# Layer 0 of a four-layer graph network: a fourth buffer for a tile's own rows, and the scatter of a tile's finished rows written inside the next tile's loop over runs

## The chip, the cores and the metric

The kernel runs on one core of a Trainium2 chip. The metric is the device time of one execution, in microseconds (us), given as the median of several executions. The engines are named as the profile names them: PE multiplies matrices, DVE works on vectors, ACT applies activations and copies, POOL issues the indexed transfers here, and SP issues the plain ones. Each engine takes its instructions in one fixed order that is settled when the program is built, and waits on semaphores for the others.

## The reference, cut to what matters

3125 nodes with rows of 128 numbers pass through four graph layers over the same 100000 edges; after each layer the result is added to its input and normalised. The layer that is touched here is the first, an attention layer with 8 heads:

```python
pre_edge = hP1[dst] + hP2[src] + zP3[edge_type]
logit_edge = _leaky(pre_edge) @ y_w
...
alpha = ex / denom[dst_a]
t_edge = hWh[src] + zWz[edge_type]
msg = (alpha[:, :, None] * t).reshape(-1, D)
agg = jax.ops.segment_sum(msg, dst_a, num_segments=n)
out = _leaky(agg + residual_weight * h)
x = _layernorm(x + out)
```

Each node also attends to itself; `denom` is the softmax's sum over a node's incoming edges and itself.

## The kernel before, in words

Nodes are sorted by their number of incoming edges and cut into 25 tiles of 128. A tile's edges fill `CAP[t]` slots for each node, from 57 in the first tile to 21 in the last, and the slots are worked in chunks of up to eight; consecutive chunks form a run.

Layer 0 loops over the tiles t:

1. `own(t + 1)` (L796) fetches the next tile's own rows: POOL clears a buffer `x` (L798) and issues an indexed gather into it (L799, recorded under the helper's line L102). Rows beyond the real nodes stay zero. There are three such buffers, so the memset of tile t + 3 needs the buffer of tile t back. The last to read `x` of tile t is the DVE instruction at L1024, which forms `y`.
2. For every chunk POOL issues up to eight gathers of neighbours' rows, `hs`, one for each slot (L102). Eight `hs` buffers are in use in turn. A chunk of the "gathered" kind also gathers rows of the relation table, `zs`, with two buffers; a chunk of the "multiplied" kind gets them from PE, by matmuls with one-hot matrices (L870, L879). PE adds the parts of the argument of the leaky function (L821, L883, L885), ACT applies it (L828), PE makes logits (L830).
3. After each run DVE does the softmax and the weighted sum (L904 to L914). This piece is given a high priority by `tc.high_priority(offset=AHEAD)`. Its last add, L914, gives the chunk's `hs` buffer back.
4. A tail finishes the tile: the node's attention to itself, `y` (L1024), the normalised rows `x1` (L757, in a helper; two `x1` buffers), and `put` (L105 in the helper `scatter`), an indexed scatter of the 128 rows into the table `x1_tab`, issued by POOL. Then `x1` is transposed and multiplied for layer 1.

Between the chunks the loop also hands out steps of another task, `counts`, which builds matrices of edge counts for layer 1 on DVE, ACT and PE.

The order of the instructions on each engine is not the order of the source. A scheduler goes through the source order with priorities, places an instruction when by its own reckoning its inputs and its buffer are free, and so lets POOL run ahead: it places the gathers of tile t + 2 before the scatter of tile t. What it placed is then fixed, and POOL waits in that order. All table writes of `put` are declared free of mutual order, since their nodes differ. Layer 1 and the later layers start when layer 0 has ended.

Of the kernel before, what the change touches and what calls it, by code (L numbers as in the profile page):

```python
# [8 lines left out]
F32 = mybir.dt.float32  # L9
# [9 lines left out]
P = 128  # L19
N = 3125  # L20
NT = 25
# [7 lines left out]
D = 128  # L29
# [58 lines left out]
def tile_gnn(ctx, tc, a, out):  # L88
# [12 lines left out]
    def gather(dst, table, idx, **kw):  # L101
        return G.indirect_dma_start(out=dst, out_offset=None, in_=table, in_offset=indirect(idx), **kw)  # L102

    def scatter(table, idx, src, **kw):
        return G.indirect_dma_start(out=table, out_offset=indirect(idx), in_=src, in_offset=None, **kw)  # L105

    def unordered(group, inst, reason):

        tc.declare_no_dep(inst.ins, group=group, reason=reason)
        tc.add_to_no_dep_group(group, inst.ins)  # L110
# [365 lines left out]
    od = Order("d", order_d)  # L476
# [287 lines left out]
    def put(table, o, t, rows):  # L764
        unordered(f"rows_{table.name}", scatter(table, o.ids(t), rows), "nodes differ")

    x1_tab = dram.tile([NP, D], F32, name="x1_tab")
# [8 lines left out]
    with tc.tile_pool(name="l0", bufs=2) as wp, tc.tile_pool(name="l0s", bufs=1) as sp, \  # L776
# [14 lines left out]
        def sums_of(t):  # L791
            az = wp.tile([P, D + R], F32, name="az")
            nc.sync.dma_start(az, sums_at[t])
            return az[:, :D], az[:, D:], az

        def own(t):  # L796
            x = wp.tile([P, D], F32, name="x", bufs=3)
            G.memset(x, 0.0)  # L798
            gather(x, a["x"], od.ids(t), bounds_check=N - 1, oob_is_err=False)  # L799
            return x  # L800

        def prologue(t, x):

            xT = transposed(wp, ps1, x, "xT", "misc")
            pw = ps1.tile([P, D + HC + H], F32, name="pw", tag="misc")
            T.matmul(pw, xT, w0, start=True, stop=True)
            hw = wp.tile([P, D + HC + H], F32, name="hw")
            A.activation(hw, pw, AF.Copy)
            hq = wp.tile([P, 3, D], BF16, name="hq")
            A.activation(hq[:, 0, :], pw[:, :D], AF.Copy)  # L810
            hrest = wp.tile([P, D], F32, name="hrest")
            V.tensor_sub(hrest, pw[:, :D], hq[:, 0, :])
            A.activation(hq[:, 1, :], hrest, AF.Copy)
            V.tensor_sub(hq[:, 2, :], hrest, hq[:, 1, :])
            return hw, hq
# [119 lines left out]
        steps = all_counts()  # L935
        n_steps = sum(4 + -(-CAP[t] // SG) + NCW for t in range(NT))
        done = 0.0
        x1st = own(0)
        ahead = x1st, prologue(0, x1st)
        for t in range(NT):  # L940
            n = CAP[t]
            x, (hw, hq) = ahead
            if t + 1 < NT:
                x_next = own(t + 1)
            ac, za, _ = sums_of(t)
            lg_ps = ps1.tile([P, max(CAP), H], F32, name="lg")
            zbT = wp.tile([P, P], F32, name="zbT")
            unset = True
            for run in runs(t):
                hss = []  # L950
                for s0, w, mult in run:
                    o = OFF[t] + s0
                    if s0 + w == n and t + 1 < NT:

                        ahead = x_next, prologue(t + 1, x_next)
                    if mult:
                        hs = multiplied(hq, o, w, zbT, unset, lg_ps[:, s0:s0 + w])
                        unset = False
                    else:
                        hs = gathered(hq, lambda s: srcx[:, o + s:o + s + 1], rel[:, o:o + w], w, za,  # L960
                                      lg_ps[:, s0:s0 + w])
                    hss.append((s0 - run[0][0], w, hs))

                    done += n_steps * w / NS
                    while done > 0:
                        next(steps, None)
                        done -= 1

                s0, s1 = run[0][0], sum(run[-1][:2])
                with tc.high_priority(offset=AHEAD):  # L970
                    lg = masked(lg_ps[:, s0:s1], hss, s1 - s0, mask[:, OFF[t] + s0:OFF[t] + s1])
                    corr, rest = weights(wp, lg[:, :s1 - s0], s1 - s0, H, m[:, t, :], l[:, t, :])
                    faded(ac, corr, H)
                    for q, w, hs in hss:
                        spread(ac, hs, lg[:, q:q + w], w)
                    rest()


            zaT_ps = ps1.tile([P, P], F32, name="tp", tag="misc")
            T.transpose(zaT_ps[:R], za, ident)  # L980
            zaT = wp.tile([R, P], F32, name="zaT")
            A.activation(zaT, zaT_ps[:R], AF.Copy)
            zb_ps = ps1.tile([P, 2 * D], F32, name="zb_ps", tag="misc")
            T.matmul(zb_ps, zbT, zw[:, :2 * D], start=True, stop=False)
            T.matmul(zb_ps, zaT, zw[:R, :2 * D], start=False, stop=True)
            zb = wp.tile([P, 2 * D], F32, name="zb")
            V.tensor_scalar(zb, zb_ps, od.rdeg[:, t:t + 1], None, op0=OP.mult)
            self_ = wp.tile([P, 2 * D], F32, name="self")
            V.tensor_add(self_, hw[:, D:3 * D], zb)
            V.tensor_add(self_[:, :D], self_[:, :D], hw[:, :D])  # L990
            V.scalar_tensor_tensor(self_[:, :D], self_[:, :D], 0.2, self_[:, :D], op0=OP.mult, op1=OP.max)
            sT = transposed(wp, ps1, self_[:, :D], "xT", "misc")
            sl_ps = ps1.tile([P, H], F32, name="sl_ps", tag="misc")
            T.matmul(sl_ps, sT, yw, start=True, stop=True)

            sl = wp.tile([P, H], F32, name="sl")
            V.tensor_sub(sl, sl_ps, hw[:, D + HC:])
            mf = wp.tile([P, 3, H], F32, name="mf")
            V.tensor_max(mf[:, 0, :], sl, m[:, t, :])
            V.tensor_sub(mf[:, 1, :], sl, mf[:, 0, :])  # L1000
            V.tensor_sub(mf[:, 2, :], m[:, t, :], mf[:, 0, :])
            A.activation(mf[:, 1:, :], mf[:, 1:, :], AF.Exp)
            V.tensor_mul(l[:, t, :], l[:, t, :], mf[:, 2, :])
            V.tensor_add(l[:, t, :], l[:, t, :], mf[:, 1, :])
            rl = wp.tile([P, H], F32, name="rcl")
            V.reciprocal(rl, l[:, t, :])
            V.tensor_mul(mf[:, 1:, :], mf[:, 1:, :], rl.unsqueeze(1).to_broadcast([P, 2, H]))

            def heads(ap):
                return ap.rearrange("p (h d) -> p h d", h=H)  # L1010

            ts = self_[:, D:]
            V.tensor_mul(heads(ac), heads(ac), mf[:, 2, :].unsqueeze(2).to_broadcast([P, H, D // H]))
            V.tensor_mul(heads(ts), heads(ts), mf[:, 1, :].unsqueeze(2).to_broadcast([P, H, D // H]))
            V.tensor_add(ac, ac, ts)
            V.scalar_tensor_tensor(ac, x, rw, ac, op0=OP.mult, op1=OP.add)
            V.scalar_tensor_tensor(ac, ac, 0.2, ac, op0=OP.mult, op1=OP.max)
            has = wp.tile([P, 2], F32, name="has")
            V.tensor_scalar(has[:, 0:1], od.deg[:, t:t + 1], 0.0, None, op0=OP.is_gt)
            V.tensor_scalar(has[:, 1:2], od.deg[:, t:t + 1], 0.0, 1.0, op0=OP.is_le, op1=OP.add)  # L1020

            V.tensor_scalar(ac, ac, has[:, 0:1], None, op0=OP.mult)
            y = wp.tile([P, D], F32, name="y")
            V.scalar_tensor_tensor(y, x, has[:, 1:2], ac, op0=OP.mult, op1=OP.add)  # L1024
            x1 = wp.tile([P, D], F32, name="x1")
            layernorm(wp, x1, y, t)
            put(x1_tab, od, t, x1)

            x1T = transposed(wp, ps1, x1, "xT", "misc")
            u_ps = ps1.tile([P, D], F32, name="u_ps", tag="misc")  # L1030
            T.matmul(u_ps, x1T, w1T, start=True, stop=True)
            u3 = wp.tile([P, 3, D], BF16, name="u3")
            A.activation(u3[:, 0, :], u_ps, AF.Copy)
            rest = wp.tile([P, D], F32, name="rest")
            V.tensor_sub(rest, u_ps, u3[:, 0, :])
            V.tensor_copy(u3[:, 1, :], rest)
            V.tensor_sub(u3[:, 2, :], rest, u3[:, 1, :])
            nc.sync.dma_start(u_tab[:, t * 3 * D:(t + 1) * 3 * D], u3.rearrange("p k d -> p (k d)"))
# [361 lines left out]
```

## Time and profile before

| | us |
|---|---|
| median of 3 runs | 5517.07 (5515.46 to 5533.62) |
| profiled execution, its own time | 5534.14 |
| its span | 5532.3 |
| layer 0's loop over tiles, in the span | about 204 to 2760 |
| POOL busy in the span | 2781.5 |
| gathers of `hs`: 821, busy | 834.9 |
| gathers of own rows: 25, busy | 30.9 |
| memsets of `x`: 25, busy | 5.2 |
| scatters into `x1_tab`: 25, busy | 31.6 |

The profile is of one execution. For each group of instructions it gives the busy time and the idle time of the engine just before, with the instruction that ended the wait (the releaser). "Issue" stands for idle time in which no wait is seen to end. On POOL the busy time of a transfer is that of issuing it. In the profile's names digits are cut off, so `x1` stands as `x`, and `x1_tab` as `x_tab`; `x_tab<-x` is the scatter and `x<-in_x` the gather of own rows.

### The profile page before, as it was taken

To read this page: it belongs to the slowest core of one execution; us is meant where nothing else is said; L and a number is where in the kernel's file an instruction comes from. 1 tells how busy PE (TensorE), PEld (TensorE's weight loads), DVE (VectorE), ACT (ScalarE), POOL (GpSimd) and SP (SyncE) were. 2 spreads that over 40 slices of the span, in tenths; PEclk is the share of its full clock that TensorE was granted. 3 is DMA by queue.
4 is the path that set the end of the run, shared out by engine and by line. 5 is a ranking of instruction groups with operands and counts; after the bars stand their busy time and mean duration, and the time that the engine had idled before them with its cause. 6 is when DMAs were issued, how large, how long until landed. Compare 5 with 4: busy or idle time off the path is not lost. (4 is left out here: it accounts for less than half of the span.)

```text
span 5532.3 us, 39989 instructions
## 1 busy us (share of the span) xinstructions
PE 2196.5 (40%) x12000; PEld 1407.3 (25%) x12141; DVE 3053.9 (55%) x6898; ACT 966.4 (17%) x2570; POOL 2781.5 (50%) x2897
## 2 busy tenths in 40 slices
PE   7146667556656666757681122223334000000000
PEld 5134444444434444544430011111111000000000
DVE  8336566546655656655522565565656344554555
ACT  1023323223222323322210011111111000000000
POOL 0553434444553444345105666566563676766665
PEclk9567787777777877877795555555555555555555
DMA  3422222222322222223253333333332332333322
GB/s 83 123 81 69 79 71 72 81 81 76 90 83 71 81 74 71 67 76 97 61 197 106 95 107 104 102 113 108 103 106 75 90 100 84 96 89 93 94 85 69
DMA packets 213051, 498.37 MB, mean 90 GB/s; under 512 B 62329, under 2 KB 109100, under 8 KB 208185
## 3 DMA queue, kind: packets, MB, share of 16 engines
q0 software_dynamic: 136448, 397.65, 25.2%
q1 hardware_dynamic: 76344, 97.76, 5.5%
q8 instruction: 102, 1.67, 0.1%
q14 instruction: 157, 1.29, 0.1%
HBM read 424.65 MB, written 70.63 MB: 90 GB/s over the span
## 5 line engine op out<-in xcount | busy, mean ns | idle before, releaser
L102 POOL DMA_INDIRECT hs<-h_tab,srcx x821 | 834.9, 1017 | 861.7 <-issue 474.7
L102 POOL DMA_INDIRECT kv<-kv_tab,pay_sb x821 | 781.8, 952 | 426.2 <-issue 240.6
L102 POOL DMA_INDIRECT kv<-ktv_tab,pay_sb x821 | 778.3, 948 | 331.2 <-issue 243.8
L728 DVE TENSOR_REDUCE u<-msg 128x128 f32<-128x1024 f32 (+4 forms) x228 | 384.5, 1687 | 132.4 <-remote 69.1
L879 PE MATMUL zps<-oh,zq 128*128 128x512 bf16 x1103 | 360.9, 437 | 83.9 <-DVE oh L870 61.2
L102 POOL DMA_INDIRECT zs<-z_tab,rel x205 | 209.5, 1022 | 274.0 <-DVE az L850 100.9
L830 PE MATMUL lg<-yw,low 128*128 128x8 f32 x1642 | 236.4, 271 | 165.0 <-ACT low L828 114.7
L883 PE MATMUL pre<-zT,zw 128*128 128x512 f32 x308 | 205.2, 754 | 204.4 <-ACT zT L881 114.2
L830 PEld LDWEIGHTS lg<-yw,low 128*128 128x128 f32 x1642 | 229.2, 214 | 210.9 <-ACT low L828 144.8
L1345 DVE TENSOR_TENSOR qk<-kv,qp 128x1024 f32<-128x1024 f32 (+4 forms) x114 | 126.5, 1110 | 270.1 <-DMA kv<-ktv_tab,pay_sb 245.1
L892 DVE TENSOR_TENSOR hs<-hs,t_ps 128x408 f32<-128x408 f32 (+1 forms) x231 | 121.9, 527 | 278.3 <-remote 166.8
L891 PE MATMUL t_ps<-zw,zT 128*128 128x136 f32 x1232 | 227.5, 316 | 103.2 <-DVE hs L892 69.7
L647 PE MATMUL c_ps<-c_ohs,c_ohd 128*128 128x128 bf16 x1300 | 140.3, 261 | 277.0 <-ACT c_sb L649 148.1
L724 DVE TENSOR_TENSOR msg<-kv,ex 128x1024 f32<-128x1024 f32 (+4 forms) x228 | 249.4, 1106 | 0.0
L570 DVE TENSOR_TENSOR c_ohs<-c_ends,c_up 128x1024 bf16<-128x1024 bf16 (+3 forms) x196 | 115.8, 592 | 241.9 <-remote 191.0
L623 ACT ACTIVATE c_oha<-c_oha,srclo 128x50 bf16<-128x50 bf16 (+2 forms) x821 | 202.2, 327 | 216.8 <-DVE c_oha L619 172.9
L891 PEld LDWEIGHTS t_ps<-zw,zT 128*128 128x128 f32 x1232 | 197.7, 216 | 140.4 <-DVE hs L892 77.2
L1193 DVE TENSOR_TENSOR qk<-kv,qp 128x1024 f32<-128x1024 f32 (+4 forms) x114 | 126.2, 1108 | 176.9 <-DMA kv<-kv_tab,pay_sb 166.9
L739 PE MATMUL tp<-ident,xk 128*128 128x128 f32 x100 | 43.2, 432 | 437.7 <-DVE xk L1261 157.0
L828 ACT ACTIVATE low<-pre 128x512 f32<-128x512 f32 (+2 forms) x215 | 123.2, 574 | 507.6 <-remote 228.5
L870 DVE TENSOR_SCALAR oh<-rb,relid 128x1024 bf16<-128x1024 f16 x308 | 146.1, 492 | 116.9 <-remote 80.6
L885 PEld LDWEIGHTS pre<-ident,hs 128*128 128x128 f32 x1232 | 191.4, 224 | 73.0 <-issue 72.0
(395 smaller groups left out, 5284.9 us busy)
## 6 DMA issues: line engine op xcount, KB each, us to landing
rb<-rel_tab SPq DMA_DIRECT2D x77, 256.0 KB
c_tab<-c_sb SPq DMA_DIRECT2D x25, 768.0 KB
cs<-c_tab SPq DMA_DIRECT2D x6, 3200.0 KB
hs<-h_tab,srcx POOLq DMA_INDIRECT x821
kv<-kv_tab,pay_sb POOLq DMA_INDIRECT x821
kv<-ktv_tab,pay_sb POOLq DMA_INDIRECT x821
h_tab<-h SPq DMA_DIRECT2D x25, 132.0 KB
zs<-z_tab,rel POOLq DMA_INDIRECT x205
```

What stands on the lines that cost most here:

```text
L102: return G.indirect_dma_start(out=dst, out_offset=None, in_=table, in_offset=indirect(idx), **kw)
L623: A.activation(oha[:, s, 0, :], oha[:, s, 1, :], AF.Copy, scale=srclo[:, o:o + 1])
L647: T.matmul(cps[:, j * P:(j + 1) * P], ohd[:, b // 2, :, b % 2], ohs[:, b // 2, :, b % 2], start=(i == 0), stop=(i == nb - 1))
L724: V.tensor_tensor(msg[:, :n, :].rearrange("p s (h d) -> p s h d", h=heads), val.rearrange("p s (h d) -> p s h d", h=heads), ex.unsqueeze(3 ...
L728: V.tensor_reduce(u, msg[:, :n, :].rearrange("p s d -> p d s"), AX.X, OP.add)
L830: T.matmul(lg_ps[:, s, :], low[:, s, :], yw8, start=True, stop=True)
L870: V.tensor_scalar(oh[:, :n * P], rb[:, :n * P], relid[:, i:i + 1], None, op0=OP.is_equal)
L879: T.matmul(zps, zq[:, i, 2 * R * k2:2 * R * (k2 + 1)], ohs[i][:, cols], start=(i + k2 == 0), stop=(i == NK - 1 and k2 == 1))
L883: T.matmul(pre[:, :k], zw[:, :D], zT[:, cols], start=False, stop=False)
L885: T.matmul(pre[:, s, :], hs[:, s0 + s, :D], ident, start=False, stop=(s == k - 1))
L891: T.matmul(t_ps[:, s, :], zT[:, (s0 + s) * P:(s0 + s + 1) * P], zw[:, D:], start=True, stop=True)
L1345: V.tensor_mul(qk[:, :n], kv[:, :n, :D], qp.unsqueeze(1).to_broadcast([P, n, D]))
```

## The change

`x` gets four buffers in place of three, so that the memset of tile t + 4 is the one that needs tile t's buffer. In the source, the scatter of tile t leaves its place after the normalisation; it is kept in `to_put` and written inside the loop over the runs of tile t + 1, behind the softmax of a run. The test stands within that loop and empties `to_put`, so the scatter is written at the end of the first run that comes along; in a tile with one run this is also its last. The last tile scatters at once, as before. No other line is changed.

```diff
@@ own(t)
-            x = wp.tile([P, D], F32, name="x", bufs=3)
+            x = wp.tile([P, D], F32, name="x", bufs=4)
@@ before the loop over tiles
+        to_put = None
@@ in the loop over runs of a tile, after the softmax of the run
+                if to_put is not None:
+
+                    put(x1_tab, od, *to_put)
+                    to_put = None
@@ in the tail of a tile
             layernorm(wp, x1, y, t)
-            put(x1_tab, od, t, x1)
+            if t + 1 < NT:
+                to_put = t, x1
+            else:
+                put(x1_tab, od, t, x1)
```

## The prediction

> **What bounds the kernel now.** I read the page's first part, then POOL's waits within layer 0, then the timeline of POOL around the two instructions that the change moves, and last the busy times by stretch.
>
> ```profile
> span 5532.3 us, 39989 instructions
> ...
> PE 2196.5 (40%) x12000; PEld 1407.3 (25%) x12141; DVE 3053.9 (55%) x6898; ACT 966.4 (17%) x2570; POOL 2781.5 (50%) x2897
> ```
>
> No engine is full. Layer 0's loop lies at 204 to 2760 us: the first `x` memset starts at 204.5, the last scatter at 2751.9. What POOL waits for in it (who waited, for what: us in total, times, longest):
>
> ```profile
> POOL hs L102 <- issue: 474.7, 773, 37.7
> POOL hs L102 <- PE pre L885: 165.1, 10, 59.3
> POOL x_tab L105 <- DVE x L757: 153.8, 12, 35.2
> POOL x L798 <- DVE y L1024: 123.1, 13, 16.8
> POOL zs L102 <- DVE az L850: 100.9, 13, 21.6
> ```
>
> Lines three and four are the change's target: the scatter waits for `x1`, the memset for the old owner of its buffer. Together 276.9 us of idle POOL. The question is whether a gather behind them could have gone earlier. One boundary in full, from POOL's timeline (start, duration, what, in brackets the idle time before it and what ended it):
>
> ```profile
> 1215.19 0.20 POOL L798 MEMSET x<- 128x128 f32 x1 [13.37 <-DVE y L1024]
> 1216.32 1.06 POOL L102 DMA_INDIRECT x<-in_x,node_d  x1 [0.92 <-POOL x L798]
> 1220.15 1.02 POOL L105 DMA_INDIRECT x_tab<-x,node_d  x1 [2.77 <-DVE x L757]
> 1226.96 0.97 POOL L102 DMA_INDIRECT hs<-h_tab,srcx  x1 [5.79 <-issue]
> ```
>
> After both waits are over, the gather waits 5.79 us more: it needs an `hs` buffer that the next tile's first run gives back, and POOL is eight chunks ahead, as many as there are buffers. Most boundaries look so: behind scatters at 517.60, 649.15, 996.25, 1840.60, 1927.57 and 2123.87 the next gather waits another 12.58, 6.46, 5.33, 6.80, 9.71 and 5.50 us.
>
> Late gathers would also have to hurt somebody. By stretch (PE, weight load, DVE, ACT, POOL busy; clock; DMA):
>
> ```profile
> 204.00:2760.00 2556.00, 1589.81 (x9716) 1111.34 (x9845) 1453.96 (x3795) 705.87 (x1898) 1114.73 (x1102) 0.75 0.28 78
> 1118.00:1136.00 18.00, 0.00 (x0) 0.00 (x0) 0.49 (x3) 0.00 (x0) 12.72 (x14) 0.59 0.46 129
> 1238.00:1248.00 10.00, 0.00 (x0) 0.00 (x0) 0.00 (x0) 2.85 (x11) 6.62 (x7) 0.64 0.40 107
> ```
>
> In both short stretches POOL issues gathers without a break while PE stands. These gathers are for later chunks, so PE isn't waiting for their data; some stall coincides with the bursts, and what it is this trace doesn't tell. Their number is unchanged.
>
> [...]
>
> **The change part by part.** I compared the built programs' order of instructions, before against after. PE, DVE, ACT and SP execute the same instructions in the same order in layer 0's loop and in all later layers (differences lie in a loop over crowded nodes that this input doesn't enter: all 821 `hs` gathers are the `CAP` slots). So only POOL's order and the waits can matter. POOL around the scatter of tile 4:
>
> ```
> before:  memset x(7)   gather x(7)   scatter x1(4)   hs gathers of tile 6, chunks 4 and 5
> after:   memset x(8)   gather x(8)   scatter x1(4)   hs gathers of tile 6, chunks 4 and 5
> ```
>
> *Fourth buffer.* Counts stay: 25 memsets of 0.212 us and 25 gathers of 1.23 us. The memset of x(8) with four buffers waits for `y` of tile 4, as that of x(7) did with three: own rows are now fetched one tile earlier, and the wait stands where it stood. Removed: 0 of the 123.1 us, but for two places. At 509.04 the wait of 5.70 us was x(3)'s; x(4) takes it. x(3) goes to about 350 us, without a wait: 0.2 + 1.0 + 0.6 = 1.8 us inside a burst, hidden by the 59.28 us that POOL then waits before 463.02. At 886.00 the memset waits 5.69 us with nine `hs` gathers behind it; in the new order they stand ahead of it, need only an L914 that DVE does before that `y`, and may go up to 5.7 us earlier. After them POOL waits 27.94 us at 927.91 for a `zs` buffer anyway: gain 0, at most 5.7. Two further memsets move by up to ten places, but waited for nothing (1320.99, 1522.94).
>
> *The moved scatter.* The source says "after a run of the next tile". But POOL has by then been given gathers far ahead, and the scheduler puts the scatter where its rows are ready, which in 22 of 25 cases is the same place between the same gathers; elsewhere one gather passes it. Removed: 0 of 153.8 us. Of that, 35.22, 29.12 and 22.61 us belong to the last three scatters, with no gather behind them at all. At 2659.46 one of the two gathers behind a 16.08 us wait passes ahead; its data is used in the last tile after 2700, so 0.
>
> *Why the waits can't yield.* In the program the DVE instructions that POOL waits for come in DVE's own order: `y` of the tile, its `x1`, then the L914 that frees the next `hs` buffer. DVE's order is untouched, so taking out a wait in the middle only lengthens the next one. Here the 13.37 + 2.77 us would become part of 5.79.
>
> *Added.* No instruction. At DVE, L757 must wait until the scatter two tiles back has read its `x1` buffer, as before:
>
> ```profile
> L757 DVE TENSOR_SCALAR x<-y,bn_mv,bn_rs 128x128 f32<-128x128 f32 x25 | 8.7, 347 | 0.1
> ```
>
> 0.1 us idle over 25; behind it on DVE stand the next tile's one-hots, and PE waits for those. The scatter's place holds, so this stays 0. PE loses 14 separate waits at the transposition of `x`, since an earlier gather is already implied; no row shows such a wait cost, so I take 0[...].
>
> SP's queue holds the same transfers in the same order; POOL's has the same 1101 before layer 1's memset.
>
> Sum: 5532.3 + 0 (-6 to +3) = 5532 us for the profiled span. That execution took 5534.14, which is 0.31% above the median of the three runs; on that median's scale the forecast is 5517 us.
>
> **The rivals.** *The scatter is really late, and DVE waits for it: slower.* Point of decision: a scatter that begins after DVE has reached L757 two tiles on; tiles follow at (2751.91 - 517.60)/24 = 93.1 us, so it would have to slip by about 186 us. Place: L757, 23 times. [...] For it speaks only the source; against it, that POOL's new order has the scatter ahead of the gathers it preceded before.
>
> *POOL's waits did hold gathers back: faster.* The places where the gather after memset or scatter started at once are 886.00, 2025.38, 2470.23 (6.16 + 2.58) and 2659.46: 5.69 + 12.10 + 8.74 + 16.08 = 42.6 us. Were all on the path and gone, 5474. Against: the waits at 2025.38 and 2470.23 stand unchanged in the new order, and gathers run a tile ahead of use.
>
> *The stalls fall differently: either sign.* [...] The two stalls shown cost some 28 us, and a handful that come or go would make 20 to 30 us: 5490 or 5545. For it: such stalls are frequent. Against: before's own runs, with all their jitter, lie within 18 us.
>
> **How the numbers follow.** That nothing changes, 0.74; late scatter 0.04; gathers freed 0.04; stalls redistributed beyond 0.3%, 0.18, of which 0.11 slower and 0.07 faster. 0.3%, or 16.5 us, is about what a measurement here can tell from none, since before's three runs spread by 18. Faster 0.11, same 0.74, slower 0.15. Before's spread and the -6 to +3 of the sum give 5506 to 5536 for the case of no change; the smaller of the redistributions take it to 5500 to 5538, which leaves out less than two in ten.
>
> **What would show it.** Right: POOL's waits for `y` at L798 and `x1` at L105 again about 123 and 154 us; L757 idle near 0; the last scatter of layer 0 near 2752. Wrong: those waits vanish and the `hs` rows' idle grows or layer 0 ends early; or L757 shows a wait for a scatter. A shift of over 16 us with all of POOL's waits as they were would point to the stalls.

## The result

Over twelve runs the changed kernel took 5527.56 us (5512.67 to 5548.25) and the kernel before, measured beside it, 5525.84 us (5501.53 to 5539.5). The ratio is 1.0011 with a 95% interval of 0.9995 to 1.0026: no difference, inside the forecast's range of 5500 to 5538. The 10.6 us between forecast and median are mostly those by which the kernel before itself came out above its first three runs (5525.84 against 5517.07).

The page's first part, of the changed kernel:

```profile
span 5534.7 us, 39978 instructions
...
PE 2186.7 (40%) x12000; PEld 1400.1 (25%) x12141; DVE 3051.2 (55%) x6898; ACT 966.6 (17%) x2570; POOL 2779.9 (50%) x2897
```

The profiled execution has the same busy times as before within 10 us, and its span is 2.4 us longer. POOL's waits in layer 0, 204 to 2760 us (who waited, for what: us in total, times, longest):

```profile
POOL hs L102 <- issue: 470.6, 769, 38.7
POOL hs L102 <- PE pre L885: 166.8, 10, 52.3
POOL x_tab L105 <- DVE x L757: 150.4, 12, 37.2
POOL x L798 <- DVE y L1029: 119.8, 13, 16.7
POOL zs L102 <- DVE az L850: 106.5, 13, 20.8
```

Compare lines three and four with those of before: the scatter waited 153.8 us there and waits 150.4 now, 12 times in both; the memset waited 123.1 and waits 119.8, 13 times in both (L1024 is now L1029). Neither wait that the change aims at has gone. The boundary that the prediction showed, in the timeline of POOL after the change:

```profile
1213.03 0.20 POOL L798 MEMSET x<- 128x128 f32 x1 [12.63 <-DVE y L1029]
1213.85 1.02 POOL L102 DMA_INDIRECT x<-in_x,node_d  x1 [0.62 <-POOL x L798]
1217.99 1.02 POOL L105 DMA_INDIRECT x_tab<-x,node_d  x1 [3.12 <-DVE x L757]
1224.80 0.97 POOL L102 DMA_INDIRECT hs<-h_tab,srcx  x1 [5.79 <-issue]
```

It is the same row of instructions with the same three waits, 12.63, 3.12 and 5.79 us against 13.37, 2.77 and 5.79. The memset clears the buffer of a tile one further on, and that is all. Over the whole of layer 0, PE, DVE and ACT run the same instructions in the same order in the two traces, and 23 of the 25 scatters have as many `hs` and `zs` gathers ahead of them on POOL as before; the other two have one more.

At one place the order on POOL did change, and it is a test within the change itself. The forecast said that behind the memset at 886.00 nine `hs` gathers would pass ahead and gain nothing. After the change they do stand ahead, the last of them at 887.83 (it was at 897.71), and behind them stand

```profile
894.36 0.20 POOL L798 MEMSET x<- 128x128 f32 x1 [5.58 <-DVE y L1029]
895.17 1.02 POOL L102 DMA_INDIRECT x<-in_x,node_d  x1 [0.61 <-POOL x L798]
905.35 1.01 POOL L105 DMA_INDIRECT x_tab<-x,node_d  x1 [9.16 <-DVE x L757]
928.76 1.27 POOL L102 DMA_INDIRECT zs<-z_tab,rel  x1 [22.40 <-DVE c_dig L609]
```

The next `zs` gather starts at 928.76, where it started at 927.91 before: nine gathers left some ten us earlier, and POOL reached the next one no sooner.

The group that would show a late scatter, the write of `x1` on DVE, among the groups of layer 0:

```profile
L757 DVE TENSOR_SCALAR x<-y,bn_mv,bn_rs 128x128 f32<-128x128 f32 x25 | 8.7, 348 | 6.7 <-remote 6.6
```

Its idle time is 6.7 us, of which 6.58 us stand at one place, 1329.53 us. "Remote" means that the profile shows nothing that ended the wait. The scatter of two tiles earlier had been issued at 1109.04, 220 us before, so it isn't that. Last, the busy times of layer 0 and of a stretch like those of the prediction (length, then PE, weight load, DVE, ACT, POOL, clock, DMA share, GB/s):

```profile
204.00:2760.00 2556.00, 1578.70 (x9716) 1103.00 (x9845) 1454.63 (x3800) 707.10 (x1901) 1113.69 (x1102) 0.75 0.28 77
1120.00:1138.00 18.00, 0.00 (x0) 0.00 (x0) 0.62 (x2) 0.00 (x0) 11.57 (x13) 0.50 0.41 114
```

The stall of PE under POOL's burst is there again, near its old place: in the 18 us of the second line PE is busy for 0.00 us and POOL for 11.57.

### The profile page after: what moved, and what is told of

Same layout as the page of the kernel before. It is cut to its first block, busy times and chain, and to the rows that moved or that the text cites. A ratio compares the mean times of both kernels' runs of the same rounds, so it can differ in the third digit from the quotient of the medians.

```text
span 5534.7 us, 39978 instructions
## 1 busy us (share of the span) xinstructions
PE 2186.7 (40%) x12000; PEld 1400.1 (25%) x12141; DVE 3051.2 (55%) x6898; ACT 966.6 (17%) x2570; POOL 2779.9 (50%) x2897
## 5 line engine op out<-in xcount | busy, mean ns | idle before, releaser
L892 DVE TENSOR_TENSOR hs<-hs,t_ps 128x408 f32<-128x408 f32 (+1 forms) x231 | 121.9, 528 | 294.6 <-remote 176.5
L870 DVE TENSOR_SCALAR oh<-rb,relid 128x1024 bf16<-128x1024 f16 x308 | 144.7, 488 | 111.2 <-remote 60.5
```

Of the source, the lines that this page charges most:

```text
L870: V.tensor_scalar(oh[:, :n * P], rb[:, :n * P], relid[:, i:i + 1], None, op0=OP.is_equal)
```

## The experiments

What was on trial: the theory that POOL waits for DVE in DVE's own order, so that a wait taken out goes into the next one; the rival that POOL's waits hold gathers back; the rival that a late scatter costs DVE's waiting; and the stalls. Each kernel is compared with the kernel before on the same chip. The comparisons fell on several chips, and these differ far more than the kernels do: the kernel before took 5525.84 us in the comparison above (on which chip isn't known), 5473.82 and 5476.22 on the one chip that most of the groups below ran on, and 4581.42 and 4584.05 on two further chips. Which of these a run was on is said each time; it turned out to matter. For the chip of 5474 to 5476 us there is no profile of the kernel before, so waits on it can only be set beside those of the forecast's profile (5534.14 us).

One thing bears on all the times below. An edit can change the order in which the scheduler places instructions on engines that the edit doesn't name. In the change, in its two halves and in the plain store, DVE and ACT run layer 0 in the old order, and so does PE by its weight loads. In the others they don't. Of some 3800 DVE instructions in layer 0, those that stand outside the longest row common to both orders are 273 for the plain load and for both plain transfers, 1115 for the late scatter, 783 and 1331 for seven and five `hs` buffers, and about 300 for the extra gathers and memsets. Those kernels differ from the one before by more than their edit says.

### Each half alone

```diff
-            x = wp.tile([P, D], F32, name="x", bufs=3)
+            x = wp.tile([P, D], F32, name="x", bufs=4)
```

> The fourth buffer for own rows alone, the scatter where it was. Theory: ratio 0.997 to 1.003, POOL's waits for y near 123 us. If the null result of the whole change is a gain and a loss that cancel, this one or the next lies outside.

The second kernel has the other edits of the change, and three buffers.

> The scatter written in the next tile's loop over runs alone, with three buffers for own rows. Theory: ratio 0.997 to 1.003, POOL's waits for x1 near 154 us. If the null result of the whole change is a gain and a loss that cancel, this one lies outside on the other side.

Measured, on a chip with 4581.42 us for the kernel before: the buffer alone 1.0013 (1.0006 to 1.0019), the scatter alone 1.0004 (0.9996 to 1.0012). Both lie within 0.3%, so on this chip there is no gain and loss that cancel. The sizes of the waits were missed: on this chip the memset of `x` has no idle time at all in front of it (0.0 us in both), and the scatter waits 53.1 and 51.4 us for `x1`, practically all of it in the last scatters. The section on the chips, below, reads this further. It also limits what the two runs show: a half that has no wait to remove can't show what it does where there is one, and on a chip near 5500 us the halves weren't run. There, that nothing cancels rests on the unchanged order and the unchanged waits. The 6 us by which the buffer alone is slower are measured, and unexplained.

### The waits taken out for good

Here the scatter leaves POOL, then the memset and the gather of own rows, then all three.

```diff
-            put(x1_tab, od, t, x1)
+            nc.sync.dma_start(x1_tab[t * P:(t + 1) * P], x1)
```

> The kernel before, with the scatter of layer 0 taken off POOL: SP stores the tile's 128 rows by a plain transfer into x1_tab, in the order of the tile (so the rows stand in other places than the reference has them; amounts are unchanged). PE, DVE and ACT run the same instructions in the same order. POOL loses 25 scatters, 31.6 us of issue, and the 153.8 us that it waits for x1 in front of them. Theory (POOL waits for DVE in DVE's own order, so what is taken out of one wait goes into the next): ratio 0.997 to 1.003; POOL's wait in front of hs gathers grows by some 120 to 185 us less the 87 us of the last three scatters, that is by 30 to 100 us; the last L757 of layer 0 again near 2752. Rival (POOL's waits hold gathers back): two to three of the places where the gather behind the scatter started at once are freed, 21 to 37 us faster, ratio 0.993 to 0.996.

```diff
-            G.memset(x, 0.0)
-            gather(x, a["x"], od.ids(t), bounds_check=N - 1, oob_is_err=False)
+            n = min(P, N - t * P); n < P and G.memset(x, 0.0)
+            nc.sync.dma_start(x[:n], a["x"][t * P:t * P + n])
```

> The kernel before, with the own rows fetched by SP in one plain transfer per tile, in the order of the node table, with no memset but the last tile's (so the rows are other nodes' than the reference has; amounts are unchanged). POOL loses 24 memsets, 25 gathers, 36 us of issue, and the 150.8 us of waits in front of the memsets. Theory: ratio 0.997 to 1.003, since those waits go to the next hs gathers. Rival (waits hold gathers back): the 5.69 us at 886 and the 12.10 us at 2025 come off, 6 to 18 us, ratio 0.997 to 0.999; the time spent on the issue, 36 us, comes off too if POOL's bursts are what sets PE's pace: ratio down to 0.990. A loss is possible where SP, waiting for a buffer, holds back the loads of rb: L870 would show it.

> Both of these: the own rows are loaded and the finished rows stored by plain transfers of SP (rows in other places than in the reference, in both), and POOL in layer 0 issues only gathers of hs and zs. POOL waits for neither y at L798 nor x1 at L105 any more: 276.9 us of waits and 67 us of issue are gone. Theory: ratio 0.997 to 1.003, all of it found again in front of hs and zs gathers. Rival: 42.6 us faster as worked out in the prediction, ratio 0.992; with the issue time too, down to 0.98.

All three ran on the chip with 5473.82 us for the kernel before. Store: 0.9956 (0.9942 to 0.9971). Load: 1.0021 (1.0007 to 1.0036). Both: 0.9995 (0.9982 to 1.0007). First the mechanism, at the boundary shown above. POOL's timeline with the plain store:

```profile
1174.49 0.20 POOL L798 MEMSET x<- 128x128 f32 x1 [13.12 <-DVE y L1024]
1175.30 1.01 POOL L102 DMA_INDIRECT x<-in_x,node_d  x1 [0.61 <-DVE bn_st L746]
1186.25 0.95 POOL L102 DMA_INDIRECT hs<-h_tab,srcx  x1 [9.94 <-issue]
```

with the plain load:

```profile
1214.74 0.99 POOL L105 DMA_INDIRECT x_tab<-x,node_d  x1 [18.12 <-DVE x L757]
1221.54 0.97 POOL L102 DMA_INDIRECT hs<-h_tab,srcx  x1 [5.82 <-issue]
```

and with both:

```profile
1211.67 0.95 POOL L102 DMA_INDIRECT hs<-h_tab,srcx  x1 [23.83 <-issue]
```

The wait for `x1`, taken out, goes to the next gather (5.79 becomes 9.94). The wait for `y`, taken out, goes to the scatter (3.12 becomes 18.12), and the gather behind keeps its 5.82. With neither, one wait of 23.83 us stands where there were three of 13.37 + 2.77 + 5.79 = 21.93 us: the first gather that needs a buffer from the next tile's run starts when that run gives it back, whatever POOL has to do before. Over layer 0, POOL's waits in front of `hs` and `zs` gathers are 1056.6 and 293.8 us with both edits, against 861.7 and 274.0 in the kernel before (the forecast's profile): 214.7 us more. Gone are 165.8 us in front of scatters, 150.8 us in front of memsets, less the 87 us of the last three scatters that had no gather behind them: 229.6 us. So nearly all of it is found again. The 87 us are too: POOL's first memset after layer 0 waits 98.6 and 99.5 us in the kernels without scatters, and 4.1 us before. The store alone returns less, 30.6 us in front of `hs` gathers, at the low end of what was expected, for the 79 us of scatter waits that had a gather behind them. Its layer 0 is shorter, with the last `x1` at 2677 where near 2752 was expected, but that figure was of another comparison. The loss that the plain load was said to risk, DVE waiting at L870 for `rb`, doesn't show: L870 is idle 109.9 us with it and 116.9 before.

The times are not so plain. By the rival, both edits together free most: 0.992. They measure 0.9995, but with DVE, ACT and PE in another order, so this is not the removal alone. The store alone, where only POOL's and SP's work changed, is 24 us faster, in the size that the rival gave for it and outside what the theory allowed. The load alone is 11 us slower. If these two add up, both together should be at 0.9977; 0.9995 (up to 1.0007) neither fits that well nor excludes it.

Whether earlier gathers made the store faster can be read from the traces. A gather that POOL's waits hold back costs time only where another engine then waits for its rows. In layer 0 of the kernel before, the waits of DVE that the profile puts down to rows of `hs` and `zs` are these three groups:

```profile
DVE zs L836 <- DMA zs<-z_tab,rel: 8.9, 2, 8.0
DVE hs L848 <- DMA hs<-h_tab,srcx: 5.4, 2, 3.2
DVE hs L848 <- DMA zs<-z_tab,rel: 3.8, 1, 3.8
```

That is 18.1 us, with 0.2 us more at PE, so the 42.6 us of the rival were not there to be won by earlier rows. With the plain store the same sum is 31.5 us, with the plain load 55.8, with both 56.1. The faster kernel waits more for its rows and not less, so the way that the rival names doesn't explain its 24 us. What does is not settled; see the stalls.

### The scatter made really late

```diff
@@ in the tail of a tile; `held` starts empty, and the last two are scattered behind the loop
+            if len(held) == 2:
+                t0, x0 = held.pop(0)
+                V.scalar_tensor_tensor(x0, y, 0.0, x0, op0=OP.mult, op1=OP.add)
+                put(x1_tab, od, t0, x0)
             x1 = wp.tile([P, D], F32, name="x1")
             layernorm(wp, x1, y, t)
-            put(x1_tab, od, t, x1)
+            held.append((t, x1))
```

> The kernel before, with the scatter of a tile made really late: one DVE instruction adds 0 times the y of two tiles on to its rows, and only then are they scattered, just ahead of the L757 that needs the same buffer. This is the rival of the prediction in which the scatter is late and DVE waits for it. It adds 25 DVE instructions of about 0.35 us, 9 us, most of them in DVE's idle time. [...] If POOL stands in a wait for hs with the scatter behind it, the scatter comes later still and L757 waits longer: over 100 us, ratio 1.02 or more.

Measured on the same chip: 0.9975 (0.9963 to 0.9988), 15 us faster. The group of the write of `x1`:

```profile
L757 DVE TENSOR_SCALAR x<-y,bn_mv,bn_rs 128x128 f32<-128x128 f32 x25 | 8.9, 354 | 92.4 <-DMA x_tab<-x,node_d 92.3
```

DVE does wait for the scatter, 92.3 us in all. It is at 9 places and not 23, and the longest wait is 23 us. At that one, POOL's timeline has the scatter at

```profile
1607.85 1.02 POOL L105 DMA_INDIRECT x_tab<-x,node_d  x1 [0.30 <-issue]
```

and DVE's timeline its sequel:

```profile
1610.24 0.34 DVE L757 TENSOR_SCALAR x<-y,bn_mv,bn_rs 128x128 f32<-128x128 f32 x1 [22.98 <-DMA x_tab<-x,node_d]
```

The rows had been ready since 1581.05; the scatter stood behind a burst of gathers in POOL's queue. POOL is busy with it for 1.02 us. From its start to DVE's go 2.39 us pass, and 2.38 to 2.45 at six of the eight other places (3.41 and 5.86 at the last two). So the rival's wait is real, but most of it is the scatter standing in POOL's queue: of the 92.3 us only some 22 lie behind the starts of the nine scatters. A price of it doesn't show: the kernel isn't slower but 15 us faster. This is not yet a price of nothing, since over a quarter of DVE's instructions stand in another place here, and what that gave or took isn't known. DVE is idle for over 1000 of layer 0's 2470 us in any case, so there was room for the wait.

### Fewer buffers for the neighbours' rows

```diff
@@ at both places that make an hs tile
-            hs = wp.tile([P, W, HC], F32, name="hs", bufs=8)
+            hs = wp.tile([P, W, HC], F32, name="hs", bufs=7)
```

> The kernel before with seven hs buffers in place of eight: POOL can be one chunk less ahead, so every gather that waited for a buffer is issued about one chunk of a run later, some 93 us / 5 chunks = 15 to 20 us. Theory (gathers run far enough ahead that lateness of a few us costs nothing): ratio 0.997 to 1.005. Rival (POOL's waits hold PE up): some us at each of 25 tiles, 1.01 to 1.04, with PE waiting in front of L885 and L855.

> Five hs buffers in place of eight, three chunks less ahead. A run holds up to three chunks, which give their buffers back only at its end, so POOL is then less than two runs ahead. Theory: here the lookahead is used up and PE does wait for gathers: ratio 1.02 to 1.08. If it is still within 1.005, gathers have far more room than the prediction needed.

On the chip with 5476.22 us: seven 0.9934 (0.9908 to 0.9959), five 0.9952 (0.9936 to 0.9967). For seven, neither side expected a gain of over 0.3%; for five, the theory expected a loss of 2 to 8%, and that was wrong. Both kernels are faster, by 38 and 32 us at the medians. With five buffers gathers do come late, which the group that first reads `hs` on DVE shows:

```profile
L848 DVE TENSOR_TENSOR hs<-hs,zs 128x2112 f32<-128x2112 f32 x15 | 35.4, 2358 | 68.7 <-DMA hs<-h_tab,srcx 63.6 <-DMA zs<-z_tab,rel 4.7
```

It is idle 68.7 us, against 6.8 in the forecast's profile of the kernel before. Over all of DVE, the waits for gathered rows are 152.5 us with five buffers and 41.0 with seven, where the kernel before had 18.1. So later gathers go along with a faster kernel here, which speaks against the rival of gathers held back. It doesn't follow that fewer buffers are better: 783 and 1331 of DVE's instructions moved with them, and the runs don't separate the buffers from the new order. On a chip near 4580 us this wasn't tried.

### What PE's stalls go with

Behind every second `hs` gather, one more instruction on POOL: a gather of 4 numbers a row, a gather of the whole row, or a memset.

```diff
@@ in a chunk of the gathered kind; the same in the multiplied kind
-                gather(hs[:, s, :], h_tab, idx(s))
+                gather(hs[:, s, :], h_tab, idx(s)); s % 2 and extra(idx(s))
```

> The kernel before with one further gather on POOL behind every second hs gather, of 4 numbers per row into a scratch tile that nobody reads: about 400 issues more, 1.25 us each, some 500 us of POOL's time, and hardly any bytes. It asks what the stalls of PE are that coincide with POOL's bursts. If PE stands because of POOL's issuing as such, its standing grows by about as much as POOL's bursts do, by half: some 200 to 400 us, ratio 1.04 to 1.07. If it stands because of the bytes moved, ratio under 1.01. POOL's own idle time in layer 0, 1441 us, has room for 500 us.

> The same with the whole row of 264 numbers gathered into the scratch tile, so half as many bytes again for hs. If the issuing is what counts, the time is that of the small ones within 0.5%. If bytes count, it is longer than the small ones by 1% or more.

> The kernel before with a memset of 640 numbers per partition into a scratch tile behind every second hs gather on POOL: the places of the extra small gathers, about the same POOL time each (1 us)[...]. If PE's standing comes with POOL being busy as such, the kernel is as slow as with the small gathers, ratio 1.06 to 1.09 on a chip near 5475. If it comes with the issuing of transfers, POOL's bursts are now thinned out by a quarter of the time and PE gets its turns in between: ratio 0.97 to 1.02.

On the chip with 5476.22 us: small 1.0791 (1.0717 to 1.0865), large 1.0602 (1.0569 to 1.0635). It is not the bytes: the larger transfers are the cheaper ones, by 117 us, against both expectations, and these two kernels have the same order on every engine. The 404 further gathers take 401.2 us of POOL's busy time, 993 ns each, when they are small, and 421.7 us, 1044 ns each, when they are large. In the stall shown by the prediction one gather on POOL starts 1.25 us after another (1118.74, 1119.99, 1121.24 us in the trace of before); 404 times that, the author's estimate, is 505 us. The small ones lengthen the kernel by 439 us. A plain reading would be that POOL is late with the rows that are needed. But DVE waits for gathered rows only 47.0 and 48.6 us in these two, some 30 us more than before, so that isn't most of it. "PE stands while POOL issues" fits in kind. The size is somewhat above what was expected, the new order has a share that isn't known, and why small rows cost more is open.

The memsets ran on a chip with 4584.05 us, where the expectation's condition doesn't hold: 1.0353 (1.0336 to 1.0371), 162 us for this group:

```profile
L792 POOL MEMSET scr<- 128x640 f32 x404 | 261.2, 646 | 18.8
```

They also took 0.65 us each and not the 1 us that was expected, the time of a small gather (993 ns). The stalls that the question is about aren't seen on that chip (see the section on the chips), so the run says nothing on them. What it shows is more waiting for POOL's rows: DVE's waits for them are 338.4 us, against 207.1 in the same layer without the memsets. That is 131 us more where the kernel takes 162 us longer, so POOL's time seems to be on the path there.

### The kernel before, on another chip

> The kernel before once more, for a profile on the same chip as the run beside it. Where the chip is one of those with times near 5475, layer 0's last L757 is expected near 2690 to 2750 and POOL's waits for y and x1 near 123 and 154 us; where it is one with times near 4581, near 2060, with no wait for y and some 51 us for x1.

This is the same program beside the memsets, 4580.41 us. POOL's waits in layer 0, 204 to 2053 us:

```profile
POOL hs L102 <- issue: 347.3, 735, 37.9
POOL hs L102 <- PE pre L885: 65.8, 13, 26.3
POOL zs L102 <- issue: 54.4, 179, 0.3
POOL x_tab L105 <- DVE x L757: 51.5, 2, 29.0
```

No memset waits, and the scatter waits 51.5 us, at two places. Layer 0's last `x1` is written at 2052 us and not at 2751. The next section reads it further.

## What the chips showed

The prediction had not expected this at all. The program is the same, but from 204 us to its last scatter layer 0 takes 1849 us in the profile of `before_again`, on a chip with 4580 us, against 2548 in the forecast's profile, some 700 us less. The layers behind it take 2519 against 2780 us, and what lies ahead of it 204 us in both. The waits of DVE in layer 0 tell the two profiles apart. In the forecast's, the first rows:

```profile
DVE c_ohs L570 <- remote: 191.0, 24, 26.0
DVE hs L892 <- remote: 166.8, 25, 45.1
```

In that of `before_again`:

```profile
DVE zs L836 <- DMA zs<-z_tab,rel: 95.9, 8, 17.3
DVE hs L848 <- DMA zs<-z_tab,rel: 76.6, 5, 21.7
DVE hs L892 <- PE t_ps L891: 57.9, 66, 3.2
```

In the forecast's the profile finds nothing that ended these waits, 191.0 and 166.8 us. L892 reads `t_ps`, which PE writes, and its wait, "remote" in the one profile, is put down to PE in the other (57.9 us). The trace of the kernel before says the same of the rest: all 162 such waits of DVE and ACT in layer 0 are for semaphores that only PE's instructions raise. They rise late, a median of 4.5 us and up to 37 us after the recorded end of the last PE instruction that raises them (a modelled end, by the profile's own account), so the profile gives no name. "Remote" is PE being late here.

Summed over DVE and ACT in layer 0, waits ended by "remote" come to 1314 us in the kernel before and 1238 after. On the 5475 us chip, in the order of the kernels' times, they are 1146 (seven buffers), 990 (five), 1094 (plain store), 1123 (late), 1131 (both), 1232 (plain load), 1533 and 1899 (more gathers, large and small). In the kernels on the chips near 4580 us they are below 1 us. PE itself is busy longer over the same matmuls in the forecast's profile: 1588.9 us in layer 0, against 1449.9 in `before_again`.

The granted clock is lower there too, a mean of 0.76 in layer 0 against 0.86. That the clock makes the stalls doesn't fit two readings. Behind layer 0 it is nearly the same (0.54, and 0.55 as worked out from the means of 0.686 over the span of `before_again` and 0.86 in its layer 0), and that part is 261 us longer all the same. And in the stall that the prediction showed, PE's last recorded matmul ends at 1117.6, while the clock (the third figure from the end) is full until 1121.3 and falls only then:

```profile
1117.70:1121.30 3.60, 0.00 (x0) 0.00 (x0) 0.66 (x3) 0.00 (x0) 2.69 (x4) 1.00 0.61 169
1121.50:1139.00 17.50, 0.00 (x0) 0.00 (x0) 0.63 (x3) 0.12 (x1) 10.14 (x11) 0.50 0.36 99
```

Other stalls begin at a clock that is already down (0.50 from 480 to 485 us, before PE stands for 23.8 us), so this doesn't speak for all of them.

In the profiles near 5500 us, then, PE stalls in the middle of its matmuls, and what waits for PE waits on. In the stall of the forecast's profile no matmul is recorded from 1117.6 to 1139.5 us, while POOL issues gathers. But for seven buffers, the order by these waits is the order by the median time (by the times of the profiled executions, the kernel with both plain transfers is out of place too). That is two figures going together, the waits from one execution each, and not a shown cause; what holds PE, and why on some chips only, no run here tells.

In `before_again` POOL is the one that is behind: the first things that DVE waits for are `zs` and `hs` rows from POOL's gathers, 207.1 us in all where the forecast's profile had 18.1. There `y` is ready whenever the memset comes (no wait of POOL at L798), so the fourth buffer has no wait to remove. The whole change wasn't run on such a chip.

## Why the prediction was right

*That nothing moves in the engines' order, and no wait goes.* Right: the traces have PE, DVE and ACT in the old order, and 119.8 and 150.4 us of waits where 123.1 and 153.8 stood, the last scatter of layer 0 at 2752.6 where 2751.9 stood, a span 2.4 us longer where the sum allowed -6 to +3. Luck had a part in the number: it holds where the times are like those that the forecast came from, and in the comparison they were. On two other chips the same program took 4581 and 4584 us, far outside the range.

*The fourth buffer shifts the wait by one tile.* Right: the memset at the shown boundary has the same wait in front of it. That was measured where the kernel takes about 5530 us; in `before_again` there is no such wait.

*The moved scatter stays in its place.* Right, at 23 of 25 places to the gather. The program's text said "after a run", but the order on POOL was decided by when its rows are ready.

*A wait taken out only lengthens the next.* Right within the change, at 886.00, and at the boundary shown: with all of them out, three waits of 21.93 us become one of 23.83. Over the whole layer the two edits together gave back 214.7 of 229.6 us, with DVE's order changed, and the plain store, with DVE's order kept, 30.6 of 79. So the step holds where it was needed, and is not shown to hold in full everywhere. "Most boundaries look so" was said too freely: of the 25, a further wait of over 5 us for an `hs` gather stands right behind the scatter at the seven that the prediction names.

*L757 stays free.* Right: 6.7 us at one place, none of it from a scatter.

*The 14 separate waits that PE loses.* Taken as 0, not measured apart; the whole result bounds them. Such a wait instruction in front of a transposition lasts 51 ns in the trace of before, which makes 0.7 us for 14, by estimate.

*The rival of the late scatter.* It did not occur in this change. What it would cost was the author's estimate, which no run had shown. Made to occur, the wait came to 92.3 us, at 9 places and not at the 23 that it was given, with 2.38 to 2.45 us from the scatter's start to DVE's go at seven of them. The wait was not time lost one for one here: the kernel with it was 15 us faster, by the wait and a new order together.

*The rival of gathers held back.* Its way is not borne out: in the kernel before the other engines waited only 18 us for gathered rows, the plain store's gain came with more of that wait, and five `hs` buffers made gathers late in a faster kernel. Its list of places had also left one out, the memset at 2549.45, which waited 7.93 us with a gather behind it that then started at once; with it the price would have been 50.5 us. The plain store's 24 us stay unexplained by either.

*The stalls fall differently.* This rival was given 20 to 30 us of either sign and 18%. How a change like this one would move the stalls is shown by no run. The change itself shows no more than its interval, -3 to +14 us, so the rival wasn't needed for it. The moves of +11, -15, -24 and -38 us on the 5475 us chip don't show how likely it was: in three of these four kernels many instructions of DVE, ACT and PE stand in another place, and in the fourth, the plain store, POOL had less to do. Where DVE, ACT and PE kept their order and POOL its work, in the change and its halves, nothing moved by more than 0.13%. The prediction went by a spread of 18 us over three runs of the kernel before; twelve runs spread by 38.

## What to carry to other kernels

Before a wait is taken out, look at what the next instruction in the same queue waits for: here that was a later instruction of the engine already waited for, and the wait came back in front of it, 214.7 of 229.6 us with both plain transfers, but only 30.6 of 79 with the store alone. The order of the built program shows such a place before anything runs. Ask also who waits for the work behind it: 277 us of POOL's waits were worth little here, since the others waited only 18 us for POOL's rows. When an experiment edits one engine's work, compare the order of the others before its time is read; here one small edit moved over a third of DVE's instructions, and the half per cent that came with it isn't the edit's alone. And an effect measured on one chip is to be tried on another: in the profiles of the kernel before on two chips the engines waited for different things, DVE and ACT 1314 us for PE in one, DVE 207.1 us for gathered rows in the other.

## What the runs showed of the hardware

The same program took 5525.84, 5473.82 and 4581.42 us in comparisons on different chips or at different times, the last on another chip than the second. In layer 0, DVE and ACT waited 1314 us in the profile of `before`, and not at all in that of `before_again`, for semaphores of PE that rose a median of 4.5 us after the recorded end of the last PE instruction that raises them; the granted clock was 0.76 and 0.86 there. 404 extra indexed gathers of 16 bytes a row (`more_small`) went with 439 us more, and the same number of 1056 bytes a row, in the same order (`more_large`), with 322 us. An indexed scatter of 128 rows of 512 bytes released its source 2.38 to 2.45 us after POOL began to issue it, at seven of nine places (`late_by_two`).
